# The first sequence of a Mamba, MoE and attention kernel: earlier tables and weight loads, separate halves, and dummy products on TensorE

## The chip, the cores and the metric

The kernel runs on one core of a Trainium2 chip. The metric is device time in microseconds for one execution. Its engines, as the profile names them: PE is TensorE (PEld its weight loads), DVE is VectorE, ACT is ScalarE, POOL is GpSimd, and SP is SyncE, which issues all DMA here.

## The reference

The input x has 8 sequences of 512 rows and 128 channels, in float32. Four residual layers follow one another, each on the layernorm of x:

```python
x = x + mamba(layernorm(x))      # W_in, depthwise conv of 3 + SiLU, scan over 512 steps, W_out
x = x + ffn(layernorm(x))        # router, 8 experts, all of them on every row
x = x + attention(layernorm(x))  # 16 heads of 8, masked in chunks of 10 with 25 to the left
x = x + ffn(layernorm(x))        # the same weights again

# mamba: h = x @ W_in.T; xb, zb = split(h); both: conv + silu
#   delta = clip(softplus(xb @ (W_dt @ W_x[:8]).T + b_dt)); b, c = tanh(xb @ W_x[8:].T)
#   decay = clip(exp(-delta * a)); state = decay * state + (1 - decay) * b * xb
#   y = sum_n state * c + D * xb;  out = concat(y, zb) @ W_out.T
# ffn: out = sum_e cw[e] * (silu(x @ w_gate[e]) * (x @ w_up[e])) @ w_down[e]
#   cw = softmax(x @ w_router) * softmax(x @ w_gating / 0.1), normalised over the 8 experts
```

`w_gate`, `w_up` and `w_down` are 8 x 128 x 512 (the last one 8 x 512 x 128), so each of the 24 weights is 256 KB.

## The kernel before

**Precision.** A large product is made of three fp32r products: both operands are split into a high part (a cast to fp32r) and a low part (the rest). `matmul3` (L462) issues high x high, high x low and low x high. ACT casts, and DVE or POOL subtracts (1.27 us for a tile of 128x512 on POOL). The 24 expert weights stay in SBUF, split.

**The order of the work** is made when the program is built. `Clock` (L115) holds an estimate of every instruction's cost and of each engine's end. `Lanes` (L262) holds generators, the lanes; each yields the engine that it needs next, or a condition, and `tick` (L311) resumes the lane that can start first. The order so found is the order in each engine's queue; on the chip an engine takes its queue strictly in order, and waits only for data and free buffers. `first` and `second` (L590) put a lane among the urgent ones, ahead of the others by 0.6 and 0.1 us. PSUM has eight banks; `sides` (L396) gives one to a lane while fewer than `OTHERS` = 4 are held outside the experts.

**The stages.** In the steady state PE works on the experts (`ffn_stream`, L1028: per expert and quarter of 128 hidden rows a `g`, a `u` and a `y` of three products each), while the Mamba layer of later sequences, the layernorms and, later, attention run in other lanes between them. The first sequence has nothing to run beside, so it goes through in two halves of 256 rows, and the first four experts take its first half, then its second (`passes`, L1035). These steps come before the experts:

1. `load_x` and the packed constants (`pa` at L441, `pc`, `pb`, `maskt`), one DMA each, on SP's queue. `pb` holds the router's weights, which `route_consts` (L921) copies on DVE.
2. `layernorm` (L471): statistics on DVE; variance, power and bias (`va`, `rs`, `nm`) on POOL; then `xn`, four tiles, on ACT or DVE by the planner's costs. `normalised` (L509) transposes `xn` on PE and splits it.
3. `mamba_consts` (L535): split W_in (`win`), `wdt`, `wbc`, the selectors `sel`, and `nega`, `cap`, `wxz`. ACT's function tables are loaded by `table` (L529), 1.28 us each.
4. `mamba_front` (L593) makes `h` (`mh`), then `first_halves` (L661) takes the two halves: convolution (`v`), SiLU (`xb`, `zb`), `delta` (`pde`), the rows of B and C (`rows_bc`, L643), `spread` products `mbx` and `mcc` that copy one row of them over the partitions, decays (`dec`) on ACT, clips on DVE, scans (`st`), products with C (`mcx`), and `mo`, the output projection. Both halves share the tiles `v`, `xb`, `zb` and `delta`, and x is loaded a second time for the residual (`x_mo`).
5. `ffn_prep` (L930): layernorm of a half, the routing logits (`lps`), the softmaxes, the weights of the experts per row (`cw`) by way of DRAM.
6. Beside these, `ffn_weights` (L880) loads the 24 expert weights through three staging tiles (`t0`, `t1`, `rest`): the load of a weight waits until the one three before it has been split.

The main loop (L1563 to 1568) starts the lanes and idles until the first half is ready for the experts.

Of the kernel before, what the change touches and what calls it, by code (L numbers as in the profile page):

```python
# [96 lines left out]
OTHERS = 4  # L97
SECOND = 0.1
# [5 lines left out]
SPLIT = 4  # L104

# [9 lines left out]
class Clock:  # L115
# [29 lines left out]
    def cost(self, key, name, out, args, kw):  # L145
# [32 lines left out]
        if key == "P":  # L178
            if ALU.pow in args:
                return 0.3 + n * 0.18  # L180
            return max(0.09 + n / 427, 0.19)
# [166 lines left out]
def block_kernel(ctx: ExitStack, tc: tile.TileContext, x, pack_a, pack_b, pack_c, w_qkv, mask, mask_t, w_o,  # L348
# [47 lines left out]
    def sides(*tiles):  # L396
        while not bank("others", OTHERS, len(tiles)):
            yield lambda: bank("others", OTHERS, len(tiles))
        return take("others", *zip(*tiles))
# [46 lines left out]
    sp.dma_start(out=pb, in_=pack_b)  # L446
    maskt = const.tile([QMAX, LEFT + QMAX], F32, name="maskt")
    sp.dma_start(out=maskt, in_=mask)
# [13 lines left out]
    def matmul3(dst, w, v, start=True, stop=True, after=0.0):  # L462

        pe.matmul(dst, w[0], v[0], start=start, stop=False, after=after)
        pe.matmul(dst, w[0], v[1], start=False, stop=False)
        return pe.matmul(dst, w[1], v[0], start=False, stop=stop)
# [4 lines left out]
    def layernorm(xc, tag, nt=NT):  # L471
# [19 lines left out]
        pool.tensor_tensor(nm, mv[:, :nt, 0], rs, ALU.mult)  # L491
        pool.tensor_scalar(nm, nm, -1.0, 1.0, ALU.mult, ALU.mult)
        for t in range(nt):
            yield "AV"
            a = max(clock.end["A"], clock.based("A")) + 0.39
# [13 lines left out]
    def normalised(xc, tag, halves, nt=NT, give=True):  # L509

        yield "V", xc[1]
        xn = yield from layernorm(xc, tag, nt)
# [22 lines left out]
    def mamba_consts(sb, mc):  # L535
        table("natural_log_exp_and_others", 6)
        route_consts()
        yield "A", pa_there
        mc["win"] = yield from split_const(pa[:, A_WIN : A_WIN + P], P, "win", sb)

        yield "T", pc_there
        wp = yield from side([P, P], "wdt_ps")
        pe.matmul(wp, pc[:, 0:P], pc[:, P : 2 * P], start=True, stop=True)
        wdt = sb.tile([P, P], F32, name="wdt", bufs=1)
        yield "V"
        freed(dve.tensor_copy(wdt, wp))
        mc["wdt"] = wdt


        wbc = sb.tile([P, P], F32, name="wbc", bufs=1)  # L550
        pick = sb.tile([P, L], F32, tag="dec", name="pick", bufs=5)[:, : 2 * DSTATE]
        yield "V"
        dve.tensor_copy(
            wbc.rearrange("p (c n) -> p c n", c=4), pa[:, None, A_PBC : A_PBC + 32].to_broadcast([P, 4, 32])
        )
        mc["wbc"] = wbc
        dve.tensor_tensor(pick, ident[:, : 2 * DSTATE], ident[:, 32 : 32 + 2 * DSTATE], ALU.add)
        yield "P"
# [6 lines left out]
        mc["sel"] = sel.rearrange("p n s c -> p n (s c)")  # L565

# [3 lines left out]
        yield "A"  # L570
        act.activation(sp_, alog, AF.Abs)
        act.activation(sp_, sp_, AF.Exp, scale=-1.0)
        act.activation(sp_, sp_, AF.Ln, bias=1.0)
        yield "V"
        dve.scalar_tensor_tensor(sp_, alog, 0.0, sp_, ALU.max, ALU.add)
        dve.tensor_scalar(nega, sp_, 1e-4, -1.0, ALU.add, ALU.mult)
        yield "A"

        cap = sb.tile([P, NSTEP], F32, name="cap", bufs=1)
        act.activation(cap, nega, AF.Exp, scale=1e-4)  # L580
        yield "V"
        dve.tensor_scalar(cap, cap, 1.0, None, ALU.min)
        mc["nega"], mc["cap"] = nega, cap

        wxz = sb.tile([P, P], F32, name="wxz", bufs=1)
        act.activation(wxz[:INNER], pa[:INNER, A_WOUT : A_WOUT + P], AF.Copy, scale=pa[:INNER, A_D : A_D + 1])
        mc["wxz"] = wxz, act.copy(wxz[INNER:], pa[INNER:, A_WOUT + P : A_WOUT + 2 * P])

# [4 lines left out]
    def mamba_front(b, sb, consts, xc):  # L593
# [7 lines left out]
        xt = yield from normalised(xc, f"m{b}", halves)  # L601
# [3 lines left out]
        if b == 0:  # L605
            first_halves(sb, consts, h)
            return
# [53 lines left out]
    def first_halves(sb, consts, h):  # L661
# [3 lines left out]
        v = sb.tile([P, L], F32, tag="v", name="mv0", bufs=1)  # L665
        xb = sb.tile([P, L], F32, tag="xb", name="mxb0")
        zb = sb.tile([P, L], F32, tag="zb", name="mzb0")
        delta = sb.tile([P, L], F32, tag="dec", name="mdelta0", bufs=5)
        xo = now(load_x(0, 0, "mo0"))
# [4 lines left out]
        def half(c):  # L674
            cs = slice(c * HALF, c * HALF + HALF)
            a, z = max(cs.start, 1), min(cs.stop, L - 1)
            yield "A"
            table("silu_and_others", 18)
            act.activation(v[:, cs], h[:, cs], AF.Copy, scale=kc[1])
            yield "V"  # L680
            dve.scalar_tensor_tensor(
                v[:, a : cs.stop], h[:, a - 1 : cs.stop - 1], kc[0], v[:, a : cs.stop], ALU.mult, ALU.add
            )
            yield "V"
            e = dve.scalar_tensor_tensor(
                v[:, cs.start : z], h[:, cs.start + 1 : z + 1], kc[2], v[:, cs.start : z], ALU.mult, ALU.add
            )
            if c:
                freed(e)
            yield "A"  # L690

            there = act.activation(xb[0:INNER, cs], v[0:INNER, cs], AF.Silu)
            there2 = act.activation(xb[INNER:P, cs], v[0:INNER, cs], AF.Silu)
            yield "T", there2
            pde = yield from side([P, HALF], f"mde0_{c}")
            hs = slice(INNER * c, INNER * c + INNER)
            pe.matmul(pde, consts["wdt"][hs], xb[hs, cs], start=True, stop=True)
            z_there = []
            bc, bc_there = yield from rows_bc(
                0, sb, consts, xb[:, cs], HALF, lambda: z_there.append(act.activation(zb[:, cs], v[:, cs], AF.Silu)), c  # L700
            )
            issued["tanh"] += 1
            yield "V"

            there = freed(dve.tensor_scalar(delta[:, cs], pde, bdt, LN_E_1, ALU.add, ALU.min))
            add[c](scanned(c, bc, bc_there, there, z_there[0]))

        def scanned(c, bc, bc_there, delta_there, z_there):
            cs = slice(c * HALF, c * HALF + HALF)
            bbs, decs, scans = {}, {}, {}  # L710

            def inputs():

                for p in range(2):
                    yield "T", bc_there
                    bx = yield from side([P, 2, HALF], f"mbx0_{c}_{p}")
                    for i in range(2):
                        e = spread(bx[:, i], consts, bc, 2 * p + i, 0)
                    yield "V", e
                    bbs[p] = bx  # L720
                    bbs["x", p] = dve.tensor_tensor(
                        bx, bx, xb[:, None, cs].to_broadcast([P, 2, HALF]), ALU.mult
                    )

            def steps():
                yield lambda: issued["tanh"] == 2
                yield "A", delta_there
                nega, cap = consts["nega"], consts["cap"]
                table("natural_log_exp_and_others", 6)
                act.activation(delta[:, cs], delta[:, cs], AF.Exp)  # L730
                act.activation(delta[:, cs], delta[:, cs], AF.Ln, bias=1.0)
                for p in range(2):
                    yield "A"
                    dec = sb.tile([P, 2, HALF], F32, tag="dec", name=f"mdec0_{c}_{p}", bufs=5)
                    for i in range(2):

                        decs["t", p, i] = act.activation(
                            dec[:, i], delta[:, cs], AF.Exp, scale=nega[:, 2 * p + i : 2 * p + i + 1]
                        )
                    decs[p] = dec  # L740
                if c:
                    table("exp_and_others", 0)
                for p in range(2):
                    dec = decs[p]
                    for i in range(2):
                        yield "V", decs["t", p, i]
                        n = 2 * p + i
                        dve.tensor_scalar(dec[:, i], dec[:, i], cap[:, n : n + 1], 1e-4, ALU.min, ALU.max)
                    yield lambda: ("x", p) in bbs
                    yield "V", bbs["x", p]  # L750
                    bx = bbs[p]

                    dve.scalar_tensor_tensor(bx, dec, 1.0, bx, ALU.subtract, ALU.mult)
                    yield lambda: c == 0 or ("st", p) in states
# [9 lines left out]
                    if c == 0:  # L764
                        yield "A"
                        states["st", p] = sb.tile([P, 2], F32, name=f"mlast{p}", bufs=1)
                        act.copy(states["st", p], st[:, :, HALF - 1])

            add[c](inputs())
            add[c](steps())  # L770

            yield "T", max(z_there, consts["wxz"][1])
            ops = yield from sides(*(([P, DIM], f"mo0_{2 * c + t}") for t in range(2)))
            tiles = [slice(cs.start + t * P, cs.start + t * P + P) for t in range(2)]
            for t, ts_ in enumerate(tiles):
                pe.matmul(ops[t], zb[:, ts_], consts["wxz"][0], start=True, stop=False)
            for p in range(2):
                yield lambda: p in scans
                yield "T", bc_there
                cc = yield from side([P, 2, HALF], f"mcc0_{c}_{p}")  # L780
                for i in range(2):
                    e = spread(cc[:, i], consts, bc, 2 * p + i, 1)
                yield "V", max(scans[p][1], e)
                cx = sb.tile([P, 2, HALF], F32, tag="acc", name=f"mcx0_{c}_{p}")
                e = freed(dve.tensor_tensor(cx, cc, scans[p][0], ALU.mult))
# [7 lines left out]
            yield "V", xo[1]  # L793
# [86 lines left out]
    def ffn_weights(sb):  # L880
# [4 lines left out]
        def load(i):  # L885
            e, nm, src = todo[i]
            t = qp.tile([P, FF], F32, tag=("t0", "t1", "rest")[i % 3], name=f"stage{nm}{e}")
# [9 lines left out]
        def loads():  # L897
            for i in range(len(todo)):
                if i > 2:
# [4 lines left out]
        split = {}  # L904
        lanes.add(loads())
        for i, (e, nm, _) in enumerate(todo):
            yield lambda: i in stages
            t, there = stages.pop(i)
            hi, lo = wgt[nm, e]
# [3 lines left out]
            act.copy(hi, t)  # L913
            yield "PV"
            split[i] = quicker(L, W_BIAS).tensor_tensor(lo, t, hi.bitcast(F32), ALU.subtract)
            done[nm, e] = 0.0
# [746 lines left out]
```

## Time and profile before

| | us |
|---|---|
| three runs | 1394.45, 1395.56, 1395.86 |
| median | 1395.56 |
| the profiled execution: time | 1394.65 |
| the profiled execution: span in the trace | 1392.8 |
| PE busy in the span | 1345.2 (97%), 8302 products |
| DVE, ACT, POOL busy | 1052.8, 963.7, 942.2 |
| first product of the experts | 47.62 |
| PE busy in 0 to 20, 20 to 40, 40 to 60 us | 7.37, 10.87, 18.41 |

How to read the profile: times are microseconds from the span's start. A line of the timeline gives start, duration from the first to the last of a merged group, engine, line, operation, names (result, then operands), shapes and count; in brackets stands how long the engine had been idle before it, and whose result ended that. Nearly all instructions are issued by one helper, so the line is L251 for all of them, and the names tell them apart. A product on PE is a weight load (LDWEIGHTS, engine PEld) and a MATMUL; a float32 product leaves two records of each, an fp32r product one, though the profile writes f32 for both. A line of the windows gives a stretch, its length, busy time and instructions of the engines named, the clock granted to PE (1.00 is full), the busy share of DMA, and GB/s. The end of a MATMUL is modelled.

### The profile page before, as it was taken

To read this page: it belongs to the slowest core of one execution; us is meant where nothing else is said; L and a number is where in the kernel's file an instruction comes from. 1 tells how busy PE (TensorE), PEld (TensorE's weight loads), DVE (VectorE), ACT (ScalarE), POOL (GpSimd) and SP (SyncE) were. 2 spreads that over 40 slices of the span, in tenths; PEclk is the share of its full clock that TensorE was granted. 3 is DMA by queue.
4 is the path that set the end of the run, shared out by engine and by line. 5 is a ranking of instruction groups with operands and counts; after the bars stand their busy time and mean duration, and the time that the engine had idled before them with its cause. 6 is when DMAs were issued, how large, how long until landed. Compare 5 with 4: busy or idle time off the path is not lost. (4 is left out here: it accounts for less than half of the span.)

```text
span 1392.8 us, 25585 instructions
## 1 busy us (share of the span) xinstructions
PE 1345.2 (97%) x8302; PEld 1074.7 (77%) x8302; DVE 1052.8 (76%) x3084; ACT 963.7 (69%) x1677; POOL 942.2 (68%) x1058
## 2 busy tenths in 40 slices
PE   4879999999999999999999999999999999999997
PEld 2767778778777878788788787787877888787886
DVE  5687778787888767888888888888888888754443
ACT  6568586768776557767777677777777776765654
POOL 3667667676666657666767667676776676777776
PEclk9699999999999999999999999999999999999999
DMA  3322122414212433456545555455564545222111
GB/s 98 97 73 52 44 58 58 118 38 122 60 40 54 74 70 65 84 111 126 129 87 126 100 114 143 79 118 118 105 140 78 117 64 103 49 66 53 39 39 39
DMA packets 257160, 116.55 MB, mean 84 GB/s; under 512 B 108012, under 2 KB 252929, under 8 KB 257025
## 3 DMA queue, kind: packets, MB, share of 16 engines
q1 hardware_dynamic: 257025, 114.90, 38.0%
q8 instruction: 66, 1.08, 0.3%
q14 instruction: 69, 0.57, 0.1%
HBM read 82.48 MB, written 31.98 MB: 82 GB/s over the span
## 5 line engine op out<-in xcount | busy, mean ns | idle before, releaser
L251 POOL TENSOR_TENSOR h<-h,h 128x512 fp32r<-128x512 f32 (+1 forms) x511 | 645.1, 1271 | 296.8 <-ACT h L251 254.1
L251 PE MATMUL u<-xt_f,wu 128*128 128x512 f32 (+1 forms) x1584 | 460.0, 399 | 7.4 <-ACT h L251 6.4
L251 PE MATMUL y<-h,wd 128*128 128x512 f32 (+1 forms) x1584 | 449.3, 393 | 8.4 <-ACT h L251 3.9
L251 PE MATMUL g<-xt_f,wg 128*128 128x512 f32 (+1 forms) x1584 | 454.9, 395 | 0.3 <-DVE mv L251 0.2
L251 ACT CAST h<-h 128x512 fp32r<-128x512 f32 (+1 forms) x476 | 285.8, 606 | 217.0 <-DVE h L251 214.6
L251 DVE TENSOR_TENSOR h<-u,h 128x512 f32<-128x512 f32 (+1 forms) x441 | 294.2, 672 | 174.5 <-PE u L251 114.2
L251 ACT ACTIVATE h<-g 128x512 f32<-128x512 f32 (+1 forms) x528 | 305.9, 584 | 113.1 <-PE g L251 81.3
L251 PEld LDWEIGHTS y<-h,wd 128*128 128x128 f32 x1584 | 291.2, 189 | 76.9 <-POOL h L251 4.7
L251 PEld LDWEIGHTS u<-xt_f,wu 128*128 128x128 f32 x1584 | 284.6, 190 | 72.8 <-ACT h L251 9.7
L251 PEld LDWEIGHTS g<-xt_f,wg 128*128 128x128 f32 x1584 | 288.6, 190 | 67.3 <-issue 2.5
L251 POOL TENSOR_TENSOR acc<-acc,cwb 128x512 f32<-128x512 f32 (+1 forms) x115 | 146.8, 1276 | 47.6 <-DVE cwb L251 27.1
L251 DVE CUSTOM_DVE_ANT_0 amasked<-as,maskt 100x125 f32<-100x125 f32 (+2 forms) x640 | 141.9, 280 | 9.1 <-PE as L251 8.6
L251 ACT ACT_TABLE_LOAD x100 | 128.3, 1283 | 15.7 <-PE g L251 14.2
L251 DVE TENSOR_TENSOR apt<-aw,maskk 125x400 f32<-125x400 f32 (+2 forms) x160 | 89.9, 576 | 12.1 <-PE aw L251 12.0
L251 DVE TENSOR_TENSOR cwb<-y,cwb 128x512 f32<-128x512 f32 (+1 forms) x115 | 77.3, 672 | 8.6 <-PE y L251 7.3
L251 ACT ACTIVATE apt<-apt 125x400 f32<-125x400 f32 (+2 forms) x160 | 80.8, 540 | 0.4
L251 DVE SCALAR_TENSOR_TENSOR h<-h,g 128x512 f32<-128x512 f32 (+1 forms) x87 | 57.5, 661 | 17.6 <-ACT h L251 17.4
L251 DVE SCALAR_TENSOR_TENSOR h<-u,h 128x512 f32<-128x512 f32 (+1 forms) x87 | 57.7, 665 | 4.0 <-DVE h L251 0.5
L251 PEld LDWEIGHTS <-ks 68*125 68x125 bf16 (+2 forms) x640 | 47.3, 136 | 10.7 <-issue 2.1
L251 PEld LDWEIGHTS <-qs 65*100 65x100 bf16 (+2 forms) x640 | 45.3, 125 | 11.1 <-issue 0.7
L251 DVE DVE_READ_ACCUMULATOR2_ANT amx<- 100x1 f32 (+2 forms) x640 | 52.4, 82 | 0.0
L251 PE MATMUL aw<-qs,ks 68*125 68x100 bf16 (+2 forms) x640 | 49.2, 220 | 0.1
(191 smaller groups left out, 1215.9 us busy)
## 6 DMA issues: line engine op xcount, KB each, us to landing
cwb<-cwd_f SPq DMA_DIRECT2D x124, 256.0 KB
aqd<-apc SPq DMA_DIRECT2D x64, 192.0 KB
ks<-aqd SPq DMA_DIRECT2D x48, 125.0 KB
qs<-aqd SPq DMA_DIRECT2D x48, 100.0 KB
x_fo<-x SPq DMA_DIRECT2D x16, 256.0 KB
aqd<-apc SPq DMA_DIRECT2D x32, 128.0 KB
x_f<-x SPq DMA_DIRECT2D x15, 256.0 KB
aod<-aos SPq DMA_DIRECT2D x24, 100.0 KB
```

What stands on the lines that cost most here:

```text
L251: f(*args, **kw)
```

## The change

What it does, by parts:

- **Loads.** The first ten expert weights get staging tiles of their own (the buffers `h0` and `h1`, which the experts' hidden rows use later), so that thirteen loads can be issued without waiting for a split. `pb` is loaded behind the first three weights, the mask at the start of attention. The second load of x goes.
- **Splits.** The low parts of the weights move into a lane of their own, `lows`; until the experts begin they run on POOL only.
- **Constants.** `sel` is made first, on POOL, from the identity. `wbc` moves from DVE to POOL, `wdt` from DVE to ACT. The table for SiLU is loaded when the constants are done, instead of at the first half's start. `wxz` and the route's constants come after h.
- **Layernorm.** With `quick`, the four `xn` of the first sequence and the two of each half go to DVE, and POOL does not make `nm`.
- **Halves.** Each half has its own tiles for `v`, `xb`, `zb` and `delta`, and its steps are split into the lanes `rows`, `inputs`, `decays`, `clips`, `steps` and `last`. B's and C's rows are spread over the partitions as soon as there are banks: outside lanes may hold seven banks (`AT_FIRST`) until the experts begin.
- **matmul3** issues high x high, low x high, high x low.
- **Dummies.** While the first half is not ready, PE gets a product of the identity with 64 of its columns (result `warm`, never read) whenever the planner has nothing to do and its own clock is past 6.0 (`WARM`). The built program has 175 of them, all ahead of the experts' first product.
- The planner's cost of a copy on POOL falls from n/427 to n/985.

The diff, cut to its core:

```diff
+AT_FIRST = 7
+WARM = 6.0
+EARLIEST = 2 * (DEPTH + 1)
...
     def sides(*tiles):
-        while not bank("others", OTHERS, len(tiles)):
-            yield lambda: bank("others", OTHERS, len(tiles))
+        while not bank("others", OTHERS if "first" in done else AT_FIRST, len(tiles)):
+            yield lambda: bank("others", OTHERS if "first" in done else AT_FIRST, len(tiles))
...
     pb = const.tile([P, B_COLS], F32, name="pb")
-    sp.dma_start(out=pb, in_=pack_b)
     maskt = const.tile([QMAX, LEFT + QMAX], F32, name="maskt")
-    sp.dma_start(out=maskt, in_=mask)
...
         pe.matmul(dst, w[0], v[0], start=start, stop=False, after=after)
-        pe.matmul(dst, w[0], v[1], start=False, stop=False)
-        return pe.matmul(dst, w[1], v[0], start=False, stop=stop)
+        pe.matmul(dst, w[1], v[0], start=False, stop=False)
+        return pe.matmul(dst, w[0], v[1], start=False, stop=stop)
...
-        pool.tensor_tensor(nm, mv[:, :nt, 0], rs, ALU.mult)
-        pool.tensor_scalar(nm, nm, -1.0, 1.0, ALU.mult, ALU.mult)
+        if not quick:
+            pool.tensor_tensor(nm, mv[:, :nt, 0], rs, ALU.mult)
+            pool.tensor_scalar(nm, nm, -1.0, 1.0, ALU.mult, ALU.mult)
         for t in range(nt):
-            yield "AV"
-            a = max(clock.end["A"], clock.based("A")) + 0.39
+            yield "V" if quick else "AV"
+            a = INF if quick else max(clock.end["A"], clock.based("A")) + 0.39
...
         table("natural_log_exp_and_others", 6)
-        route_consts()
-        yield "A", pa_there
-        mc["win"] = yield from split_const(pa[:, A_WIN : A_WIN + P], P, "win", sb)
+        pool.tensor_tensor(pick, ident[:, : 2 * DSTATE], ident[:, 32 : 32 + 2 * DSTATE], ALU.add)
...
         act.activation(cap, nega, AF.Exp, scale=1e-4)
+        table("silu_and_others", 18)
+
+        yield "T", pc_there
+        wp = yield from side([P, P], "wdt_ps")
+        pe.matmul(wp, pc[:, 0:P], pc[:, P : 2 * P], start=True, stop=True)
+        wdt = sb.tile([P, P], F32, name="wdt", bufs=1)
+        yield "A"
+        freed(act.copy(wdt, wp))
...
-        v = sb.tile([P, L], F32, tag="v", name="mv0", bufs=1)
-        xb = sb.tile([P, L], F32, tag="xb", name="mxb0")
-        zb = sb.tile([P, L], F32, tag="zb", name="mzb0")
-        delta = sb.tile([P, L], F32, tag="dec", name="mdelta0", bufs=5)
-        xo = now(load_x(0, 0, "mo0"))
+        vs = [sb.tile([P, L], F32, tag=tag, name=f"mv0_{c}", bufs=n)[:, :HALF] for c, (tag, n) in enumerate((("v", 1), ("st", 2)))]
+        xbs, zbs, deltas = [
+            [sb.tile([P, L], F32, tag=tag, name=f"m{tag}0_{c}")[:, :HALF] for c in range(2)] for tag in ("xb", "zb", "acc")
+        ]
+        done["halves"] = 0.0
...
+            add[c](rows())
             add[c](inputs())
+            add[c](decays())
+            add[c](clips())
             add[c](steps())
...
-            t = qp.tile([P, FF], F32, tag=("t0", "t1", "rest")[i % 3], name=f"stage{nm}{e}")
+            if i < EARLIEST:
+
+                t = fp.tile([P, L], F32R, tag=f"h{i % 2}", name=f"stage{nm}{e}", bufs=DEPTH + 1).bitcast(F32)
+            else:
+                t = qp.tile([P, FF], F32, tag=("t0", "t1", "rest")[i % 3], name=f"stage{nm}{e}")
...
+        def lows():
+            for i, (e, nm, _) in enumerate(todo):
+                yield lambda: i in stages and len(stages[i]) == 3
+                yield lambda: "halves" in done and "quiet" not in done if i < EARLIEST else "first" in done
+                t, there, _ = stages.pop(i)
+                hi, lo = wgt[nm, e]
+                yield "PV" if "first" in done else "P", there
+                engine = quicker(L, W_BIAS) if "first" in done else pool
+                split[i] = engine.tensor_tensor(lo, t, hi.bitcast(F32), ALU.subtract)
+                done[nm, e] = 0.0
+            done["weights"] = 0.0
+
+        for i in range(3):
+            load(i)
+        sp.dma_start(out=pb, in_=pack_b)
         lanes.add(loads())
+        lanes.add(lows())
...
         clock.hold = INF
+
+        warm = now(side([P, L], "warm"))
         while (0, 0) not in ready or ready[0, 0][1] == 0:
-            lanes.idle()
+            if lanes.tick():
+                continue
+            if clock.now > WARM:
+                e = pe.matmul(warm[:, :INNER], ident, ident[:, :INNER], start=True, stop=True)
+            else:
+                clock.now += 0.03
+        freed(e)
```

## The prediction

> **What bounds the kernel now.** I read the page's slices first, then the table of windows, the timeline of the first 60 us, the list of who waited for whom, and last single weight loads.
>
> The page: TensorE (PE) is short of work only at the start.
>
> ```profile
> PE   4879999999999999999999999999999999999997
> PEclk9699999999999999999999999999999999999999
> ```
>
> The windows of 20 us (length, then busy time per engine, granted clock, DMA) say it in numbers. From 200 us on PE is busy throughout, so the end moves by what the start gains or loses, and little else.
>
> ```profile
> 20.00:40.00 20.00, 10.87 (x42) 9.07 (x40) 17.05 (x35) 13.20 (x28) 7.95 (x8) 0.72 0.32 95
> 40.00:60.00 20.00, 18.41 (x108) 15.92 (x108) 12.38 (x46) 9.46 (x25) 11.45 (x22) 0.69 0.28 79
> ...
> 200.00:220.00 20.00, 20.00 (x89) 15.68 (x88) 15.73 (x33) 14.89 (x25) 15.67 (x20) 1.00 0.13 28
> ```
>
> In the timeline the experts' first product starts at 47.62 us, right behind the routing logits; I call this moment E. PE's longest wait before it is for VectorE (list of waits).
>
> ```profile
> 46.60 1.10 PE L251 MATMUL lps_f<-xt_f,route 128*32 128x128 f32 x8 [0.46 <-ACT xt_f L251]
> 47.62 1.01 PE L251 MATMUL g<-xt_f,wg 128*128 128x256 f32 x3
> ```
>
> ```profile
> PE mo L251 <- DVE mcx L251: 10.2, 4, 7.9
> ```
>
> **The change, part by part.** It shortens the chain to E (VectorE, ScalarE, GpSimd), and it puts 175 dummy products into PE's queue ahead of E. In the changed program's order their groups are 12, 5, 16, 19 and 10 up to the first half's spreads, then 5, 21, 16, 5, 7, 5, 9, 30 and 15. Only the first dummy waits (for the identity); all others run in order as fast as PE takes them, and every real product waits behind them.
>
> *One dummy.* It is float32, 128 weight columns by 64 moving columns. A float32 product is two records, each with its own load:
>
> ```profile
> 4.62 0.49 PEld L251 LDWEIGHTS wdt_ps<-pc 8*128 8x128 f32 x2 [4.62 <-DMA pc<-in_pack_c]
> ```
>
> Two cuts of the timeline give a load of 128 columns at full clock: the first starts at 92.59, the next cannot start until 92.70, when the first has been taken over.
>
> ```profile
> 92.59 0.19 PEld L251 LDWEIGHTS u<-xt_f,wu 128*128 128x128 f32 x1 [1.47 <-ACT h L251]
> ...
> 92.70 0.30 PEld L251 LDWEIGHTS u<-xt_f,wu 128*128 128x128 f32 x2
> ```
>
> So 0.11 us per load and 0.22 per dummy. At half clock one load ends 0.29 after 49.50, two end 0.50 after it; a later load there takes 0.333 (tile view of pa, median), so the second began 0.17 after the first: 0.33 per dummy.
>
> ```profile
> 49.50 0.29 PEld L251 LDWEIGHTS g<-xt_f,wg 128*128 128x128 f32 x1
> ...
> 49.50 0.50 PEld L251 LDWEIGHTS g<-xt_f,wg 128*128 128x128 f32 x2
> ```
>
> The other bound: 128 moving columns take 0.225 per product (101.71 to 101.94 below); if 64 cost half, a dummy is 0.11, which is about what the planner charges it (64 x 4 / 2400 + 0.01 = 0.117). I take the loads, since they are the same size in a dummy, and keep 0.11 for a rival.
>
> ```profile
> 101.71 0.31 PEld L251 LDWEIGHTS mo<-wxz,mzb 128*128 128x128 f32 x2
> 101.94 0.30 PEld L251 LDWEIGHTS mo<-pa,macc 128*128 128x128 f32 x2
> ```
>
> The Trainium skill ("TensorE: Matmul & The Clock Gate", Back-to-back issue gap) gives a gap of moving columns / 2.4 GHz plus 2.5 ns; at two passes of 128 cycles this would make a dummy 0.11 and the change a gain. Its section on LDWEIGHTS gives columns / 1.2, or 0.107 per load, and 0.21 per dummy. The row at 92.59 agrees with the second.
>
> *The clock.* Stretches of 3.41 us, with PE's busy time and the clock granted in them:
>
> ```profile
> 35.48:38.89 3.41, 2.69 (x13) 0.50 0.58 155
> 38.89:42.31 3.42, 2.64 (x13) 0.50 0.20 75
> 45.72:49.13 3.41, 2.95 (x16) 0.50 0.60 165
> 49.13:52.55 3.42, 3.42 (x16) 0.50 0.25 70
> 52.55:55.96 3.41, 3.41 (x32) 1.00 0.01 2
> 90.09:93.50 3.41, 2.03 (x13) 1.00 0.66 188
> 93.50:96.92 3.42, 1.76 (x8) 1.00 0.01 2
> 96.92:100.33 3.41, 3.02 (x14) 0.50 0.01 2
> ```
>
> A stretch busy for 79% leaves the clock at half, a full one opens it; once open, 2.03 us keep it and 1.76 lose it. (Before 25 us the page shows 1.00, but products ran at half: two of 256 columns take 0.43, 23.98 to 24.41.) A cold dummy moves columns for 2 x 0.107 of its 0.33 us (half of the 0.21 that 128 columns take there), 65%: too little by these rows. The first dense stretch is that of the spreads and the second half's projections (3.4 us), so I let the clock open there. Afterwards dummies move columns for 48% of the time, between what held the clock and what lost it, and I let it stay.
>
> The skill's rule (same page, Part 1) opens the gate after one busy window of 3.4 us. If dummies count as busy, that is at some 7 us, the first rival's case below.
>
> *PE up to E.* Start 1.4 (identity made at 1.00 + 0.29). At half clock: 62 dummies x 0.33 = 20.5; the wdt product 0.4, four transposes 0.85, mh 3 x 0.43 = 1.3, four float32 products of 256 columns x 0.85 = 3.4, eight spreads x 0.21 = 1.7, together 7.7. That is 29.6. At full clock: 113 x 0.22 = 24.9; twelve mo products x 0.225 = 2.7, eight spreads x 0.12 = 1.0, transposes and logits 0.6, together 4.2. **E = 58.7, 11.1 later than now.**
>
> *The shorter chain, hidden by that.* Route no longer stands ahead of the statistics (VectorE waited to 5.12 for pb; pa, behind x in the queue, was there at 4.36): 0.8 or more. The four xn move from ScalarE (1.65) to VectorE behind rs, without two GpSimd steps (0.4). The table load of 13.17 leaves the path (0.6), the halves no longer share v, xb and zb, and the first half's VectorE work is ahead of the second's (x_mo added at 38.3 now). With the rows' durations, and PE taken as never late: x there at some 4.0; statistics 1.1, rs 1.4, four xn 1.4 (0.34 each, the shortest xn of VectorE in the trace), transposes and both xt 1.6, mh 0.4 beyond them: 9.9. Convolution of the first half 2.0, a cast 0.6, two Silu 0.9, projections 0.9: 14.3. Tanh 0.8, zb 0.4, the other half's Silu 0.9, a cast 0.6, its tanh and zb 1.2, table 1.3: ScalarE at 19.5. Exp, Ln and two decays 1.7, clip, product, scans 2.7, mcx 0.7: 24.6. The second pair 2.7, PE 1.1: 28.4. x added and statistics 1.2, rs behind a split 2.1, xn 0.7: 32.4. Two clips, a product and two scans stand ahead of xt on VectorE (2.8), xt 0.4, logits 0.3: 35.9, and 1 for the clips held up by splits (below): **E = 37**, 10.6 earlier than now. This cover is 20 us thick where dummies are slow; without it these numbers are the result (second rival).
>
> *Loads and splits.* Thirteen loads of 256 KB leave at once; x, pa, pc, pb, mask and three weights (1.4 MB) took from 2 to 7.3 us, so ten more take some 10 and are there by 18, while ScalarE casts the last at about 32. pb passes three loads (3 us) and is needed at E. One load of x falls away. The splits on GpSimd (1.27 each, 13 of them) lie beside the chain but hold VectorE's clips up: two took 1.62 beside one split, 0.75 without. That, and a split that starts right after rs while xn waits, costs 1 to 2 us in the chain, none while PE is behind.
>
> ```profile
> 36.07 1.62 DVE L251 TENSOR_SCALAR mdec<-mdec,cap 128x256 f32<-128x256 f32 x2
> 36.26 1.28 POOL L251 TENSOR_TENSOR wg<-stageg,wg 128x512 fp32r<-128x512 f32 x1 [0.85 <-ACT wg L251]
> ```
>
> *After E.* The experts no longer start at half clock: 47.62 to 52.55 was worth 2.5, a gain. VectorE has the logits' copy, a product, two scans and statistics (some 6.5 us) ahead of freeing the second bank, PE work for 4.7: 0 to 2 lost, taken as 0. The other order in matmul3 changes no load count; the low part is needed one product later, worth at most 0.23 where y waited for it (three waits). The stops at 82.7 (3.9, ScalarE's run of decays) and 90 to 97 (VectorE) come from sequence 1, whose instructions follow in the same order; a new plan can move them by 4 either way, nothing by itself.
>
> Sum against the profiled execution (span 1392.8, time 1394.65): 1394.65 + 11.1 - 2.5 = 1403.3. The median of the runs is 0.9 above that execution: **1404**.
>
> **Rivals.** *The clock opens at once.* Cold dummies count as busy: 17 at 0.33, 158 at 0.22 (40.4), other products 8.2, start 1.4: E = 50. Then 2.4 - 2.5: **1395.5**, no change. For it: dummies leave PE no gap. Against: the 79% rows.
>
> *Dummies are cheap (the other side: faster).* At 0.117 with the clock open all groups end before their inputs come, E = 37 by the chain: -10.6 - 2.5 + 2 (the stop after E is then real): **1384.5**. It decides from 0.22 downwards: with the clock open at once E is 50 there, just no gain, and each 0.01 less is 1.75 us. Against: every load behind a wait shows 0.11; for it: a load not behind a wait might hide its first part.
>
> *The clock never opens before E.* 175 x 0.33 = 57.8, other products 15.9, start 1.4: E = 75, the experts start cold as now: **1423**. For it: 48% lies near the 1.76 us row.
>
> **How the numbers follow.** Forecast 0.45 (1396 to 1410 by where the clock opens, by the 4 us of plan and 2 of stop), cheap dummies 0.22, clock at once 0.20, never 0.13. What a measurement of this kernel can tell from no change is 0.2%, or 2.8 us. Faster: 0.22, 0.07 of the clock-at-once case and 0.03 of the forecast's tail, 0.32; same: 0.11 and 0.05, 0.16; slower 0.52. The range 1383 to 1417 leaves out half of the cheap case's spread and most of the last case.
>
> **What would show it.** Dummies' load spacing: 0.11 or 0.055 at full clock. PEclk before E, and product lengths. E in the timeline: 37, 50, 59 or 75. If PE waits for VectorE ahead of tp_f, the chain rules; if xn lies ready for 5 us or more, the dummies do. Wrong would be: a load hidden behind another, a stop after 60 us that a new plan makes or takes away.

## The result, and the profile after

The changed kernel took 1430.38 us (median of six runs, 1428.51 to 1446.38) against 1395.71 before: a ratio of 1.0282 over all runs, with a 95% interval of 1.0225 to 1.0339 (the two medians alone give 1.0248). Four runs lie between 1428.5 and 1431.8, two at 1446.2 and 1446.4. The profiled execution took 1428.91, with a span of 1427.1, which is 34.3 more than before.

The page's slices again, TensorE (PE) and its clock:

```profile
PE   9987999999999999999999999999999999999998
PEclk9998999999999999999999999999999999999999
```

PE is now busy from the start, and the clock is shown as nearly full. Neither means work: the windows of 20 us (length, busy time per engine, granted clock, DMA) show who pays.

```profile
20.00:40.00 20.00, 20.00 (x82) 17.40 (x82) 5.38 (x12) 9.35 (x21) 3.81 (x3) 1.00 0.00 0
40.00:60.00 20.00, 20.00 (x95) 20.00 (x95) 7.03 (x12) 7.69 (x17) 3.77 (x3) 1.00 0.00 1
60.00:80.00 20.00, 20.00 (x172) 19.73 (x171) 10.30 (x20) 0.76 (x2) 5.85 (x6) 1.00 0.14 41
...
200.00:220.00 20.00, 19.40 (x88) 15.39 (x87) 14.15 (x32) 18.00 (x29) 11.39 (x12) 1.00 0.28 79
```

From 20 to 40 us VectorE (the third busy time) fell from 17.05 us of work to 5.38: it waits. PE starts only 82 and 95 records in these windows and 172 in the next (the counts in brackets are records, two for a float32 product). Twice as many in the same time would fit a clock that doubled between them; the spacing of the loads, below, shows it. The column of the granted clock says 1.00 there all the same: the trace has no clock record before 62.69, and the view then shows full speed. Ahead of the first record the counts and the spacing have to be read instead.

The list of who waited for whom, VectorE's waits up to 80 us:

```profile
DVE x_m L254 <- PE mo L254: 14.8, 2, 14.7
DVE mbx L254 <- PE mbx L254: 7.6, 2, 4.1
DVE macc L254 <- PE mde L254: 7.2, 1, 7.2
```

Before, PE waited for VectorE (10.2 us for `mcx`); now VectorE waits for PE. The timeline of PE says what PE is doing:

```profile
40.20 9.06 PE L254 MATMUL warm<-ident 128*128 128x64 f32 x42
49.02 0.77 PE L254 MATMUL mbx<-mbc,sel 128*128 128x256 f32 x2
...
68.13 6.81 PE L254 MATMUL warm<-ident 128*128 128x64 f32 x60
74.78 0.39 PE L254 MATMUL tp_f<-ident,xn_f 128*128 128x128 f32 x2
75.01 3.46 PE L254 MATMUL warm<-ident 128*128 128x64 f32 x30
78.40 0.63 PE L254 MATMUL lps_f<-xt_f,route 128*32 128x128 f32 x8
78.96 0.62 PE L254 MATMUL g<-xt_f,wg 128*128 128x256 f32 x3
```

Real products stand behind groups of dummies (each dummy is two records), and not one of them has an idle time in brackets. The experts' first product, E, starts at 78.96 in place of 47.62: 31.3 of the 34.3 us.

Their weight loads give the price of a record:

```profile
39.99 9.08 PEld L254 LDWEIGHTS warm<-ident 128*128 128x128 f32 x42
48.95 0.55 PEld L254 LDWEIGHTS mbx<-mbc,sel 128*128 128x128 f32 x2
...
68.03 6.78 PEld L254 LDWEIGHTS warm<-ident 128*128 128x128 f32 x60
74.67 0.26 PEld L254 LDWEIGHTS tp_f<-ident,xn_f 128*128 128x128 f32 x2
```

From the start of a group to the start of what follows: 42 records in 8.96 us, or 0.213 each, and 60 in 6.64, or 0.111 each. A dummy costs 0.427 at half clock and 0.222 at full. The change of pace falls into the middle of the groups at 62.7 us, seen in stretches of 3.41 us:

```profile
55.96:59.37 3.41, 3.41 (x17) 1.00 0.00 0
59.37:62.79 3.42, 3.42 (x19) 1.00 0.00 0
62.79:66.20 3.41, 3.41 (x33) 1.00 0.00 0
```

### The profile page after: what moved, and what is told of

The parts are those of the page before. It is cut to its first block, busy times and chain, and to the rows that moved or that the text cites. A ratio compares the mean times of both kernels' runs of the same rounds, so it can differ in the third digit from the quotient of the medians.

```text
span 1427.1 us, 26280 instructions
## 1 busy us (share of the span) xinstructions
PE 1398.9 (98%) x8652; PEld 1133.1 (79%) x8652; DVE 1050.4 (74%) x3090; ACT 963.2 (67%) x1671; POOL 945.0 (66%) x1057
## 5 line engine op out<-in xcount | busy, mean ns | idle before, releaser
L254 DVE SCALAR_TENSOR_TENSOR h<-h,g 128x512 f32<-128x512 f32 (+1 forms) x90 | 58.4, 651 | 18.5 <-ACT h L254 18.2
L254 PEld LDWEIGHTS warm<-ident 128*128 128x128 f32 x350 | 63.6, 283 | 2.4 <-POOL ident masks.py:199 1.3
L254 PE MATMUL warm<-ident 128*128 128x64 f32 x350 | 63.9, 367 | 1.3 <-POOL ident masks.py:199 1.3
```

The lines of the kernel that those rows point to most:

```text
L254: f(*args, **kw)
```

## The experiments

In the first five, all instructions but the dummies stand in the order of the change: `pe.real.matmul` issues a dummy past the planner, and `clock.run` charges the planner for it as before. Times are medians; the ratio to the kernel before, measured on the same chip, is over all runs, with its 95% interval.

**No dummies.**

```diff
-                e = pe.matmul(warm[:, :INNER], ident, ident[:, :INNER], start=True, stop=True)
+                e = clock.run("T", "matmul", warm[:, :INNER], (warm, ident), {}, 0.0, 0.0)
```

> The 175 dummy products are not issued; the planner still charges their cost, so every other instruction stands where the change has it. Theory (the dummies hold PE back, 0.427 us each at half clock, 0.222 at full): without them E, the first product of the experts (78.96 in the changed kernel), is set by the chain, 37 to 40 us. The experts then start at half clock, as before the change. Time 1394.65 - 9 + the 5.5 that the changed kernel lost behind E (34.3 in all, 31.3 up to E, less 2.5 for a warm start) = 1391, 1385 to 1394. Rival (the chain itself became longer, by GpSimd's splits or by the seven banks): E stays at 50 us or more, and PE waits for VectorE or ScalarE for 5 us at a time; 1400 or more.

Measured: 1394.01, ratio 1.0004 (0.9992 to 1.0016); E = 42.20.

```profile
42.20 1.01 PE L254 MATMUL g<-xt_f,wg 128*128 128x256 f32 x3
```

Without the dummies E comes 36.8 us earlier, so it was they that held PE. But E is 2 to 5 later than expected, the time stands at the upper end of the theory's range, and a chain that is 5.4 shorter up to E gave no shorter kernel.

**Thin dummies**, 32 weight columns.

```diff
-                e = pe.matmul(warm[:, :INNER], ident, ident[:, :INNER], start=True, stop=True)
+                pe.real.matmul(warm[:32, :INNER], ident[:, :32], ident[:, :INNER], start=True, stop=True)
+                e = clock.run("T", "matmul", warm[:, :INNER], (warm, ident), {}, 0.0, 0.0)
```

> The dummies have 32 weight columns in place of 128; their 64 moving columns, their number and the order stay. Theory (a dummy's time is that of its two weight loads, 0.213 each at half clock for 128 columns): with a quarter of the columns the moving columns decide, 0.107 per record at half clock and 0.053 at full, and PE's stream is dense, so the clock opens within the first two or three stretches of 3.41 us. All groups of dummies end before their inputs come; E = 37 to 40; the experts start at full clock. 1394.65 - 9 - 2.5 + 5.5 = 1389, 1382 to 1392. Rival (a load takes the same whatever its columns are): E stays near 79, the records stay 0.213 and 0.111 apart, 1428. Second rival (the clock counts weight columns too, and does not open): E some 45 to 50, 1400.

Measured: 1391.90, ratio 0.9979 (0.9967 to 0.9992); E = 40.20; records 0.107 apart at half clock and 0.056 at full; the clock opened at 9.1.

```profile
32.70 3.38 PEld L1623 LDWEIGHTS warm<-ident 128*32 128x32 f32 x60
...
40.20 0.63 PE L254 MATMUL g<-xt_f,wg 128*128 128x256 f32 x3
```

The same 175 products with a quarter of the weight columns take half the time and warm the clock. Both rivals fall. The planner's charge of 0.117 was right for this dummy (0.112), not for the one in the change.

**Thin dummies of 128 moving columns** (`warm[:32, :P], ident[:, :32], ident`).

> 32 weight columns and 128 moving columns: by the theory a dummy is as long as now (two records of 0.213 at half clock, 0.107 at full), but its time is stream and not load. It tells whether the clock follows the stream. Theory: it opens by 8 us; then 17 dummies cost 7.3, 158 cost 33.7, the other products 9, start 1.4: E = 51; 1394.65 + 4 - 2.5 + 5.5 = 1402 (1397 to 1406). Rival (the clock does not care for the dense stream, and opens at 62.7 as in the changed kernel, or later): E = 79 or 94, 1428 or 1446.

Measured: 1406.25, ratio 1.0082 (1.0062 to 1.0102); E = 54.89; clock open at 6.2; records 0.109 apart. The theory holds for the clock and the spacing; I had E 4 too early, and the time stands at the end of the range, 0.25 past it.

**16 moving columns** (`warm[:, :16], ident, ident[:, :16]`).

> 128 weight columns, but 16 moving columns in place of 64. Theory (the loads set the length): records stay 0.213 us apart at half clock. There is a quarter of the stream, so the clock should not open before E; then 350 records x 0.2133 = 74.7, other products at half clock 18, start 1.4: E = 94, and the experts start at half clock: 1427 + 15 + 2.5 = 1445 (1442 to 1449), the same as the two runs of the changed kernel at 1446.2 and 1446.4, which would be runs in which the clock did not open at 62.7. Rival (the moving columns set the length): records come 0.06 apart or less, E = 37 to 45, under 1395.

Measured: 1444.85, ratio 1.0365 (1.0341 to 1.0388); E = 93.66. Tile view of `warm` (duration min/median/max in ns, first and last start):

```profile
L1623 PEld LDWEIGHTS warm<-ident x350: 287/333/339, 1.3 to 92.1; 128*128 128x128 f32 x175
```

and its last dummies and E in the timeline:

```profile
86.09 6.42 PE L1623 MATMUL warm<-ident 128*128 128x16 f32 x30
...
93.66 1.01 PE L254 MATMUL g<-xt_f,wg 128*128 128x256 f32 x3
```

Last load at 92.1. A quarter of the moving columns saves nothing: the spacing stays at 0.213 (all of it at half clock), and the clock does not open before 95.86, behind E. So the length is the load's, and a PE that loads without pause but streams little stays at half clock.

**The old weights, 128 moving columns** (`warm[:, :P], ident, ident`): twice the products per dummy.

> The dummies keep their 128 weight columns and move 128 columns in place of 64, so each asks for twice the products. Theory (length = the longer of load and stream; the clock follows the stream): the stream of a record, 0.213 at half clock, now equals its load, so a dummy takes no longer than in the changed kernel (0.427 and 0.222), but the stream has no gaps and the clock opens in the first stretches: E = 55 as with 32 weight columns and 128 moving ones (54.89), time 1406 (1402 to 1410), 24 less than the changed kernel for twice the dummy work. Rival (it was the number of weight columns that kept the clock at half): E stays at 79 to 94 or goes above, 1428 or more.

Measured: 1402.84, ratio 1.0052 (1.0035 to 1.0069); E = 51.86; clock open at 4.8.

```profile
40.94 6.86 PE L1623 MATMUL warm<-ident 128*128 128x128 f32 x60
47.64 0.38 PE L254 MATMUL tp_f<-ident,xn_f 128*128 128x128 f32 x2
```

The last 60 records take 6.70 us, 0.112 each: as long as with 64 columns. Twice the work, and 25.8 us less than the change on the same chip (1428.63, below), because the stream has no gaps and opens the clock at once.

**The old order in `matmul3`**, on top of the thin dummies.

```diff
-        pe.matmul(dst, w[1], v[0], start=False, stop=False)
-        return pe.matmul(dst, w[0], v[1], start=False, stop=stop)
+        pe.matmul(dst, w[0], v[1], start=False, stop=False)
+        return pe.matmul(dst, w[1], v[0], start=False, stop=stop)
```

> The thin dummies (32 weight columns, 64 moving), and matmul3 back in the old order: high x high, high x low, low x high. All else stays in order. A part of the loss behind E (the thin version is 7.4 earlier at E and starts at full clock, but ends only 3.3 earlier) would come from this order if theory A holds: 2 us or more less than the thin version's 1391.9. Theory B (the order only moves which operand is needed last): the y products need the low part of h one product earlier, three waits for GpSimd by 0.1 to 0.2 each; the same within 1 us, 1391 to 1393.

Measured: 1392.02, ratio 0.9980 (0.9968 to 0.9992), against 1391.90 of the thin version; E = 41.39 in the profiled run. Theory B; the order is worth nothing that shows.

**The fourth expert's casts behind xt**, on top of the thin dummies: `EARLY = 3` in place of 5, which lets ScalarE cast these weights only after the transposed xn.

> The thin dummies, and the casts of the fourth expert's weights on ScalarE stand behind the cast of the transposed xn in place of ahead of it; their splits on GpSimd, which need them, therefore cannot run beside xn, the clips and xt on VectorE. Theory (GpSimd's splits hold VectorE up): the two xn, 2.5 us in the thin version and in the one without dummies, take 0.75 to 0.9 (0.74 for one is the row behind E), the clip behind them 0.35 in place of 1.36, so E = 40.2 - 2.6 = 37.6. The end gains less than that, since the stops behind E lie with VectorE and ScalarE: 1389 to 1392. Rival (xn is slow for another reason): xn stays at 2.5 and E at 40.

Measured: 1389.98, ratio 0.9959 (0.9943 to 0.9974); E = 38.65. VectorE and GpSimd in the thin version:

```profile
33.05 1.27 POOL L254 TENSOR_TENSOR wg<-stageg,wg 128x512 fp32r<-128x512 f32 x1
33.12 2.51 DVE L254 TENSOR_SCALAR xn_f<-x_m,mv_f,rs_f 128x128 f32<-128x128 f32 x2 [0.34 <-POOL rs_f L254]
34.27 1.27 POOL L254 TENSOR_TENSOR wu<-stageu,wu 128x512 fp32r<-128x512 f32 x1
35.50 1.26 POOL L254 TENSOR_TENSOR wd<-staged,wd 128x512 fp32r<-128x512 f32 x1
35.55 1.36 DVE L254 TENSOR_SCALAR mdec<-mdec,cap 128x256 f32<-128x256 f32 x1
```

and with the casts moved:

```profile
32.99 0.60 DVE L254 TENSOR_SCALAR xn_f<-x_m,mv_f,rs_f 128x128 f32<-128x128 f32 x2 [0.34 <-POOL rs_f L254]
33.51 0.35 DVE L254 TENSOR_SCALAR mdec<-mdec,cap 128x256 f32<-128x256 f32 x1
```

Two xn fall from 2.51 to 0.60 and a clip from 1.36 to 0.35: beside a split, each of these small operations had lasted as long as the split (1.27). E moved by 1.6 and not by 2.6, because tp_f, ready at 33.6, started at 36.04 behind 30 dummies.

**The change once more, unaltered.**

> The changed kernel as it is, once more. Theory (the clock opens at 62.7 or not before E, which decides 17 us): the runs fall in two groups, 1428 to 1432 and 1444 to 1448, and the profiled one shows the clock at half up to some 62 us with E at 79, or up to E at 93 to 94. Rival (another cause for the two runs at 1446): a profile of a long run would have E at 79 and lose the time behind it, or times would lie between the groups.

Measured: 1428.63 (four runs, 1428.12 to 1429.36), ratio 1.0238 (1.0214 to 1.0261); E = 78.06, clock open at 60.8. No run was long this time, so no profile of one exists. That the two at 1446 are runs in which the clock stayed at half until E is inferred from the run with 16 moving columns, which did so and took 1444.85.

**Fewer late dummies**: as the version with the casts moved, but of the last 45 dummies only every third. The part of its diff that does this:

```diff
...
+                n_warm += 1
+                if n_warm <= 130 or n_warm % 3 == 0:
+                    pe.real.matmul(warm[:32, :INNER], ident[:, :32], ident[:, :INNER], start=True, stop=True)
...
```

> As the version with the fourth expert's casts moved (E = 38.65, 1389.98), but of the last 45 thin dummies only 15 are issued. There the transposes of xn started at 36.04, behind 30 dummies, though xn was ready at 33.6. Theory (the queue of dummies holds a real product even when it is short): tp_f starts at 33.8; xt on VectorE then waits for the two scans ahead of it (to 36.0), so E = 37.2, 1.4 earlier; the end gains that or less, 1388.5 to 1390. Rival (VectorE's scans decide alone): E stays at 38.5. The clock should stay open: the stretch before E keeps more than half of its stream.

Measured: 1388.17, ratio 0.9951 (0.9932 to 0.9971), the lowest of all; but the interval overlaps that of the version with the casts moved (0.9943 to 0.9974), so the gain shows at E and is not clear of the noise at the end. PE's timeline:

```profile
33.86 0.44 PE L254 MATMUL tp_f<-ident,xn_f 128*128 128x128 f32 x2
34.23 0.74 PE L1626 MATMUL warm<-ident 128*32 128x64 f32 x10
35.12 0.41 PE L254 MATMUL lps_f<-xt_f,route 128*32 128x128 f32 x4
36.44 0.41 PE L254 MATMUL lps_f<-xt_f,route 128*32 128x128 f32 x4 [0.90 <-DVE xt_f L254]
36.78 0.62 PE L254 MATMUL g<-xt_f,wg 128*128 128x256 f32 x3
```

PE waits 0.90 for VectorE's xt: now the chain rules, and E is 36.78.

**The second half's xn by the planner**, on the version with the casts moved: `quick=nt < NT and t0 == 0`.

> As the version with the fourth expert's casts moved, but the second half's two xn may go to ScalarE or VectorE by the planner's costs, as before the change; a new plan behind E follows from it. Theory (part of the loss behind E is the stop of 1.77 at 56, where the second transposes wait for VectorE's xn): the stop goes, and the time falls by 1 to 2, to 1388 to 1389. Rival (a stop that goes comes back elsewhere, because VectorE and ScalarE are behind there with sequence 1 in any plan): within 1 of 1390, or longer.

Measured: 1394.77, ratio 1.0000 (0.9988 to 1.0012), 4.8 longer than the version with the casts moved, so the theory falls: the stop shrank from 1.76 to 0.94 us, but the edit made a new order. Compared at equal numbers of expert products done, this version was 2.4 behind the other at 66 us, 1 ahead at 400 us and 3.5 behind at 740 us. Most of the loss lies far from the edit, so this run cannot price the stop by itself.

**The kernel before with thin dummies**: all else keeps its old order. The first part of the diff gives back the PSUM bank that `warm` takes.

```diff
     def sides(*tiles):
-        while not bank("others", OTHERS, len(tiles)):
-            yield lambda: bank("others", OTHERS, len(tiles))
+        while not bank("others", OTHERS + ("first" not in done), len(tiles)):
+            yield lambda: bank("others", OTHERS + ("first" not in done), len(tiles))
...
+        warm = now(side([P, L], "warm"))
+        last = 6.0
         while (0, 0) not in ready or ready[0, 0][1] == 0:
-            lanes.idle()
+            if lanes.tick():
+                continue
+            clock.now += 0.03
+            if clock.now > max(last + 0.117, clock.end["T"]):
+                last = clock.now
+                pe.real.matmul(warm[:32, :64], ident[:, :32], ident[:, :64], start=True, stop=True)
+        freed(clock.now)
```

> The kernel before with nothing changed but 231 thin dummies (32 weight columns, 64 moving columns) in the planner's idle time up to E; every other instruction stands in its old order. It tells what warming alone is worth. Theory A (the change's shorter chain is given back behind E, and what the repaired versions gain is the warm clock): E = 46.5, since the cold products on the chain get 1 shorter, and the experts start at full clock, worth 2.5: 1391 to 1392, as good as the change with thin dummies (1391.9). Theory B (the shorter chain is what pays): no better than 1394.

Measured: 1394.43, ratio 0.9995 (0.9982 to 1.0007); E = 46.76. That is theory B's number, but not its reading: the run without dummies had the shorter chain alone and gained nothing either (1.0004). Neither pays by itself; with both, the thin dummies in the change's order, the ratio is 0.9979. The warm start was there: at equal numbers of expert products done the version was 2.2 to 2.7 ahead from 55 to 87 us. By 150 us that was lost, as the windows show (PE's busy time and records, clock), first before, then with thin dummies:

```profile
80.00:100.00 20.00, 12.96 (x63) 0.84 0.23 65
...
120.00:140.00 20.00, 18.15 (x93) 1.00 0.10 26
```

```profile
80.00:100.00 20.00, 12.93 (x53) 0.68 0.22 63
...
120.00:140.00 20.00, 18.14 (x89) 0.96 0.13 28
```

PE is busy as long, but at half clock for more of it, and does fewer products. The stops are the same (2.2, 3.9 and 1.9 us at the same places); what differs is how many stretches of 3.41 us at half clock follow them: three before, six here, in one profiled execution of each. These executions are close in time (1394.65 and 1395.21), but the runs of the kernel before that were measured beside this version spread from 1390.71 to 1398.98, so what the one profile of it shows need not hold for all of them.

## Why the prediction was wrong, point by point

The direction and the mechanism were forecast: the dummies, not the chain, set E. The size was not: 1404 forecast, 1430 measured, outside 1383 to 1417.

**The failed step is "I let the clock open there", at the spreads.** It opened at 62.7, not at about 29.6, where the sum of the half-clock part ends, so 113 dummies ran cold and 62 warm, where I had 62 and 113. At the measured prices the 51 dummies between cost 51 x (0.427 - 0.222) = 10.5 us; what is left for the real products is 15.6 in place of 11.9, or 3.7 more. The timeline puts 2.7 of that behind the spreads, where most of them ran at half clock instead of full, and 1.7 ahead of them, where my prices were too low at half clock already; the first loads of the trains give 0.7 back.

**Why it did not open there is not settled.** My rule, that a stretch full of work opens it, is refuted by the unaltered repeat. The changes of the clock that these traces record lie a whole number of 3.41 us apart, and the repeat opened at 60.81; if the stretches ahead of the first record lie on the same grid, one of them ran from 33.50 to 36.92. In it PE had the spreads and projections only, without a gap and without a dummy, and the dummies behind still come 0.213 apart:

```profile
33.06 1.20 PE L254 MATMUL mbx<-mbc,sel 128*128 128x256 f32 x4
34.06 1.05 PE L254 MATMUL mbc<-mxb,wbc 128*128 128x256 f32 x2
35.05 1.22 PE L254 MATMUL mde<-mxb,wdt 64*128 64x256 f32 x2
36.19 1.22 PE L254 MATMUL mcx<-mbc,sel 128*128 128x256 f32 x4
37.21 2.23 PE L254 MATMUL warm<-ident 128*128 128x64 f32 x10
...
40.19 9.06 PE L254 MATMUL warm<-ident 128*128 128x64 f32 x42
```

Nor do dummies in a stretch keep it shut by themselves: the stretches that did open the clock, 59.3 to 62.7 in the change and 57.4 to 60.8 in the repeat, hold 1.6 and 1.4 us of dummies beside `mcx` and `mo`. One difference is that `mde` uses 64 rows where these products use 128; no run tests whether it matters. With a dense stream of dummies it opened at 4.8 to 9.1; with 16 moving columns not before E.

**The second one is the price at half clock, 0.33 in place of 0.427.** I subtracted the ends of a first and a second load (0.167). The dummies' first pair is 0.168 apart too, nearly all later ones 0.213. The profile before had the price as well, one load further on: three loads end 0.71 after 49.50 and two 0.50 after it, 0.21 between them.

```profile
49.50 0.71 PEld L251 LDWEIGHTS g<-xt_f,wg 128*128 128x128 f32 x3
```

On the 62 dummies that I had cold this is 6.0 us. The two steps and the real products, 20.2, are the 20.3 by which E missed; the share of the real products is what was left over, so the sum is no check of its own.

**The price at full clock held**: 0.22 forecast, 0.222 measured. The rival at 0.117 was wrong for this dummy, and the run with thin ones shows that it is the weight columns that decide. That the clock stays open at 48% of stream held as well.

**The rival in which the clock never opens** had the mechanism of the run with 16 columns and, as inferred above, of the two runs at 1446, but at the wrong price: E = 75 and 1423, against 93.66 and 1444.85. Priced at 0.427 per dummy it would have given E = 92 and 1440, and a range that reaches towards it would have held 1430.

**The chain.** E = 37 when nothing of PE stands in its way: 36.78 in the version with fewer late dummies. In the change's own order it is 40.2 to 42.2, as the splits cost more than the "1 for the clips held up by splits": 1.9 in xn and 1.0 in a clip. That version had these splits moved away, so that it agrees with 37, which has the 1 for splits in it, is partly luck.

**Behind E.** I put the warm start at -2.5 and the rest at nothing. In the kernel before with thin dummies the lead was 0.9 at E and 3.0 at 53 us, so there the warm start was worth 2.1. The rest cost 5.5 (34.3 - 31.3 + 2.5), or 5.1 with that price. The waits of PE behind E, 79 to 180 us, in the change:

```profile
PE u L254 <- DVE mst L254: 4.4, 1, 4.4
PE u L254 <- ACT h L254: 3.9, 2, 2.2
PE g L254 <- DVE mst L254: 2.8, 1, 2.8
PE tp_f L254 <- DVE xn_f L254: 2.0, 2, 1.8
```

PE's gaps in the 320 us behind E sum to 18.2 us against 15.8 before, and five stretches at half clock follow them against three (half of PE's busy time in them is 2.2 more). That comes to 4.6; the last 0.5 to 0.9 stays open. The large stops (4.2 to 4.4 and 2.7 to 2.9 us) sit 37 to 40 and 48 to 51 us behind E in all versions with this order, whether E is at 37 or at 94, so they belong to the new order and not to the dummies. Why this order has them was not settled: one edit aimed at one stop made things worse.

**The gain that went missing** in the version without dummies: 5.4 earlier at E and 0 at the end, for the same reason. The cold start is still there, as before the change; behind E PE's gaps sum to 17.4 against 15.8, and half of its busy time at half clock in six stretches, against three, is 3.6 more: 5.2 in all.

Two rules of the Trainium skill, weighed again. "TensorE: Matmul & The Clock Gate", LDWEIGHTS, gives a load as columns / 1.2, 0.107 for 128; measured are 0.111 at full clock and nearly twice that, 0.213, at half. Part 1 opens the gate of the clock after one busy window of 3.4 us, however few products it holds. The runs agree for dense streams (4.8 to 9.1 us) and not for loads with a thin stream between them, nor for the stretch from 33.50 to 36.92 above. For the splits, "SBUF — State Buffer" (section "SBUF: two separate sides") says that GpSimd and some of VectorE's operations share one pair of ports under an exclusive lock held for a whole instruction; the xn that lasts as long as the split beside it (2.51 for two, 1.27 for one split) agrees.

## What to carry to other kernels

A filler product is paid for in its engine's queue like any other, so price it by what bounds it (here two loads of 128 weight columns) and keep it thin in weights and dense in moving columns; check that it warms the clock, and that it is never longer than the wait that it fills. Read a spacing from the middle of a long train of instructions and not from its first pair. And a gain at one point of a tightly ordered program has to be followed to the end: ahead at E by 5.4 us, or by 2.2 to 2.7 with a warm clock, was worth nothing here by itself, and both together 2.8.

## What the runs showed of the hardware

- A record's spacing is the longer of load and stream: 128 weight columns 0.213 and 0.111 us (half and full clock) with 64 moving columns, 0.213 and 0.112 with 128, and 0.213 at half clock with 16 (not seen at full clock); 32 weight columns 0.107 and 0.056 with 64 moving columns, 0.213 and 0.109 with 128.
- Loads with little stream do not open the clock: 92 us of loads and products without a stop, most of them dummies with 16 moving columns, left it at half.
- A stretch of 3.41 us full of real products need not open it either: 33.50 to 36.92 in the repeat.
- With 64 moving columns it is a near thing: open at 60.8 and 62.7 in two profiles, and by the times not before E in two of ten runs.
- A stop of the same length does or does not cost a stretch at half clock: 1.9 us of waiting kept full clock before and lost it, at the same place, in the kernel before with thin dummies.
- On VectorE an xn tile of 128x128 took 1.25 beside a split on GpSimd and 0.3 without.
